# Expert tiles loaded four ahead in the first mixture, and the work beside them placed piece by piece inside tiles

## The chip, the cores and the metric

The kernel is one program on one core of one Trainium2 chip. The metric is the time of one execution on the device, in microseconds (us); lower is better. The core's engines each follow their own instruction stream: TensorE (PE, with its weight loads as PEld), VectorE (DVE), ScalarE (ACT), GpSimd (POOL) and SyncE (SP), which issues most of the transfers. They meet at semaphores.

## The reference, cut to what matters

Two layers follow each other on 4096 tokens (64 sequences of 64) of 256 numbers. Each has a sequence part (a scan and attention in the first; a recurrent net and a Mamba block in the second), whose result is added to x, and a feed-forward part. The change lies in the second layer's feed-forward part, two mixtures of experts in a row. The first has a shared part for all tokens and eight routed experts with GELU, of which each token takes two; the second has eight experts with SiLU gates, again two for each token:

```python
def _L1_cond2_ref(x, t_emb, W_router, router_bias, s_w1, s_w3, s_w2, r_w1, r_w2):
    for e in range(N_SHARED):                      # 2
        h = silu(x_flat @ s_w1[e].T) * (x_flat @ s_w3[e].T)
        shared_out = shared_out + h @ s_w2[e].T
    shared_out = shared_out / N_SHARED
    s = sigmoid(concatenate([x_flat, t_flat]) @ W_router.T)
    _, topk_idx = top_k(s + router_bias, TOP_K)    # 2 of 8
    s_sel = take_along_axis(s, topk_idx, axis=1)
    gates = s_sel / (sum(s_sel) + 1e-09)
    for e in range(N_EXPERTS):                     # 8
        h = gelu(x_flat @ r_w1[e].T, approximate=False)
        routed_out = routed_out + h @ r_w2[e].T * gates_full[:, e:e + 1]
    return (shared_out + routed_out) / (N_SHARED + TOP_K)

def _L1_ffn_ref(x, Wg, W1, W2, W3):
    topk_scores, topk_idx = top_k(xt @ Wg.T, TOP_K)      # 2 of 8
    gate = silu(einsum('td,ehd->teh', xt, W1))
    y = einsum('teh,edh->ted', gate * einsum('td,ehd->teh', xt, W2), W3)
    return einsum('te,ted->td', w, y)              # w: the two scores

x = x + _L1_attn_ref(_L1_cond_ref(x, ...), ...)
x = x + _L1_ffn_ref(_L1_cond2_ref(x, ...), ...)
return x
```

## The kernel before

Tokens are worked on in 8 chunks of 512. A mixture computes only the chosen experts: a token's row (its 256 numbers with weights, rank and number beside them) is written twice by POOL, with an indirect transfer, into the region of each of its experts (`Routing.send`, L1133, into `moe_x` or `ffn_x`). SP then loads a tile of 256 or 128 consecutive rows of one region (`Routing.read`, L1142, `gx`), with that expert's weights, chosen by a number that SP reads from a table. A tile goes through three steps on PE: `turn` (transposes of gx, L1330, copied to gxT by DVE, L1332), `up` (first products and the activation on ACT: `Gelu.up` L1421 and L1423, `Swiglu.up` L1463 to L1471) and `down` (second products, L1355, scaled by ACT at L1357). POOL scatters the result rows back by token (`give`, L1149, into `moe_y` or `ffn_y`).

The first mixture has two routings, moe0 for chunks 0 to 3 and moe1 for chunks 4 to 7, each with 16 full tiles (256 rows) and 8 half tiles (128 rows) in the order full, full, half: 48 tiles. The second has one routing for all chunks; its first 8 tiles (EARLY) come from a table made before the choice for chunks 4 to 7 is known, from what the first four chunks have sent.

All orders are written by hand. `Experts.run` is a generator: tile k+1 is turned and tile k+2's loads are issued between up and down of tile k, so loads run two tiles ahead, in pools of three buffers (`qw`, `gw`). It pauses once a tile, before up. Other work is cut in pieces by generators of its own, and `mixtures` decides how many pieces run between two tiles:

- Beside the first tiles: `Mixture.shared` for the last chunk (L1598, L1614), and `Mixture.rest`: scores of the last chunk, the choice for moe1, and the sends of chunks 4 to 7 (transposes L1580, then scatters). `send` pauses after every four scatters.
- From moe1's fourth tile on: the second mixture's gate for chunks 0 to 3. For a chunk, SP fetches the shared rows and the routed rows (L1158), DVE adds them (L1640), PE transposes the sum (L1664), ACT copies it to x2T, PE makes the scores (L1282, L1292); after every second chunk (a lot) DVE chooses the experts, two small matmuls count (L1099, L1100), and POOL scatters the lot's rows into ffn_x.
- Before the last three Gelu tiles the table of early Swiglu tiles is made (a count matmul at L1203) and Swiglu's generator is started; then the gate for chunks 4 to 7 runs between the first Swiglu tiles.

`scores`, which the gate and the mixtures use, is also used during Mamba, where pieces of the mixture's shared work and sends run beside the scans (VectorE, L916). There ACT switches between tables of functions (L884 exponentials, L762 and L1609 SiLU).

At the end the rows in ffn_y are loaded by chunks of 1 MB (`rows3`, three buffers), summed in pairs and transposed on PE (L1782), added to x by DVE (L1791) and stored.

Of the kernel before, what the change touches and what calls it, by code (L numbers as in the profile page):

```python
# [20 lines left out]
P = 128  # L21
# [1254 lines left out]
def scores(g, work, W, x, bias=None):  # L1276


    nc = g.nc
    ps = bank(g)  # L1280
    for k in range(KD):
        nc.tensor.matmul(ps[:NE, :], W[:, k, :], x[:, k, :], start=(k == 0), stop=(k == KD - 1))  # L1282
    s = work.tile([P, 2, CH // 2], F32, name="up").rearrange("p a (b l) -> p (a b) l", l=L)[:NE]
    pb = ps[:NE, :].rearrange("e (b l) -> e b l", l=L)
    if bias is None:
        nc.scalar.copy(s, pb)
    else:
        nc.vector.tensor_tensor(s, pb, bias.unsqueeze(2).to_broadcast([NE, CB, L]), ALU.add)
    s2 = s.rearrange("e b l -> e (b l)")
    pt = bank(g, (P, TT, NE))  # L1290
    for t in range(TT):
        nc.tensor.transpose(pt[:, t, :], s2[:, ts(t, P)], g.ident[:NE, :NE])  # L1292
    return pt


class Experts:
# [8 lines left out]
    def run(self, sections):  # L1305

# [64 lines left out]
        now = next(tiles)  # L1371
        load_rows(now)
        after = next(tiles)
        load_rows(after)
        turn(now)
        while now:
            yield
            self.up(now)
            if after:
                turn(after)  # L1380
            nxt = next(tiles, None)
            if nxt:
                load_rows(nxt)
            down(now)
            now, after = after, nxt
# [16 lines left out]
class Gelu(Experts):  # L1402


# [10 lines left out]
    def up(self, v):  # L1415
        nc = self.g.nc
        n = self.H // P
        ps = bank(self.g, (P, n, TR))[:, :, : v.rows]
        for j in range(n):
            for k in range(KD):  # L1420
                nc.tensor.matmul(ps[:, j, :], v.w1[:, k, ts(j, P)], v.xT[:, k, :], start=(k == 0), stop=(k == KD - 1))  # L1421
        v.h = self.p2.tile([P, n, TR], F32, name="rh")[:, :, : v.rows]
        nc.scalar.activation(v.h, ps, AF.Gelu)  # L1423

# [4 lines left out]
class Swiglu(Experts):  # L1429

# [19 lines left out]
    def up(self, v):  # L1453
# [3 lines left out]
        for i in range(full + 1):  # L1457
# [10 lines left out]
            else:  # L1468
# [6 lines left out]
                for j in range(v.S):  # L1475
                    nc.vector.tensor_mul(v.h[ts(j, H2), i, ts(j, P)], s[H2:, ts(j, P)], ps[H2:, 0, ts(j, P)])

# [9 lines left out]
class Mixture:  # L1487
# [31 lines left out]
    def beside(self, c, x, work):  # L1519

        g = self.g
        pt = scores(g, work, self.Wr[:, :KD, :], x, self.cond[:, ts(c, CB)])
        g.nc.scalar.copy(self.score[:, ts(c, TT), :], pt)
        yield
        if c == MLOT - 1:
            yield from self.choose(0, work)
        for i in self.SENDS.get(c, ()):
            yield from self.send(i, work, work)  # L1530
        if c == NCH - 2:
            self.tables = self.routings[0].tiles(self.pool)
            yield
        yield from self.shared(c, x, work)
# [88 lines left out]
    def rest(self, x, work, pool):  # L1623

        pt = scores(self.g, work, self.Wr[:, :KD, :], x, self.cond[:, (NCH - 1) * CB :])
# [6 lines left out]
    def combine(self, c, rows, work):  # L1632

        nc = self.g.nc
        nc.sync.dma_start(rows, self.made[ts(c, CH), :].rearrange("(t p) d -> p t d", p=P))
        got = work.tile([P, TT, 2, D], F32, name="rows2")
        self.routings[c // MLOT].fetch(c, got)
        yield
        for j in range(2):
            nc.vector.tensor_add(rows, rows, got[:, :, j, :])  # L1640


class Gate:
# [13 lines left out]
    def chunk(self, c, rows, work):  # L1657

        g, nc = self.g, self.g.nc
        x = work.tile([P, KD, CH], F32, name="x2T")  # L1660
# [6 lines left out]
        pt = scores(g, work, self.Wg, x)  # L1667
# [25 lines left out]
def mixtures(g, mix, x, out, last, work, close):  # L1693
# [7 lines left out]
    some = lambda pieces, n: deque(islice(pieces, n), 0)  # L1701
    with ExitStack() as ctx:
# [3 lines left out]
        first, q2, q3, qy = pool("qw", 3), pool("q2", 2), pool("q3", 2), pool("qy", 6)  # L1706
# [6 lines left out]
        n += NHT  # L1713
        others, shared = mix.rest(last, work, q3), mix.shared(NCH - 1, last, work)
        for _ in range(4):
            some(others, 1)
            some(shared, 3)
        for i in range(n - 1):
            next(tiles)
            some(others, 2)  # L1720
            some(shared, 2)
# [3 lines left out]
        next(tiles)  # L1725
        close()

        pw, p2, p3, py = pool("gw", 3), pool("g2", 2), pool("g3", 3), pool("gy", 4)
# [3 lines left out]
        def gates(chunks):  # L1732
            for c in chunks:
                rows = pg.tile([P, TT, RW], F32, name=f"x2_{c % MLOT}")
                yield from mix.combine(c, rows[:, :, :D], pg2)
                yield from gate.chunk(c, rows, pg)
# [9 lines left out]
        )  # L1746
        others = gates(range(MLOT))
        for i in range(n):
            if i > 3:
                some(others, 2)  # L1750
            if i == n - 3:
                some(others, None)
                tables2.append(routing.early(p1))
                next(tiles2)
            next(tiles, None)
        others = gates(range(MLOT, NCH))
        for i in range(EARLY - 2):
            some(others, 1 if i == 0 else 6)
            next(tiles2)
# [4 lines left out]
        next(tiles2)  # L1764
        px, close_px = scoped(tc, "gx", side="right")
        xs = []
        for c in range(NCH):
            x = px.tile([P, KD, CH], F32, name=f"x3_{c}")
            nc.sync.dma_start(x, g.x[:, :, ts(c, CH)])
            xs.append(x)  # L1770
            some(tiles2, 1)
        some(tiles2, None)
        for c in range(NCH):
            rows = px.tile([P, TT, 2, D], F32, name=f"rows3_{c % 3}")
# [161 lines left out]
```

## Time and profile before

| what | value |
|---|---|
| runs | 3056.66, 3058.62, 3066.81 us; median 3058.62 |
| profiled execution | 3053.17 us, of which the span of its instructions is 3051.3 |
| mean granted clock of TensorE | 0.907 |
| PE busy with the shared experts' first products (L1598) | 256.4 us in 896 matmuls |
| PE busy with Gelu down (L1355, tiles of r) | 86.5 us in 316 matmuls |
| PE busy with Swiglu up (L1463) | 326.6 us in 1600 matmuls |
| VectorE's scans in Mamba (L916) | 603.1 us in 512 instructions |
| POOL's scatters of Gelu results (L1149, moe_y) | 76.7 us in 79 instructions, 971 ns each |
| ACT_TABLE_LOAD at L884 | 61.6 us in 48, 1283 ns each |

In the span's own time, the layers up to the recurrent net take 0 to 827 us, Mamba 827 to 2059, the first mixture with its neighbours 2059 to about 2438, the first Swiglu tiles with the last gate chunks to 2550, the other Swiglu tiles to 2995, and the tail the rest.

In a row of an engine's timeline the first number is the start, the second the time the group of instructions took, then engine, line, operation, output and inputs, shapes and count; in square brackets stands the idle time of that engine just before, and what ended it. "Remote" means a semaphore that the trace doesn't tie to one instruction, "issue" time in which the engine waited for nothing that the profile shows. A share of the span is a mean over stages with different limits, so the table is read by stage.

### The profile page before, as it was taken

How to read it: one execution, taken by the hardware profiler on the slowest of the kernel's cores; microseconds unless marked ns; L12 is line 12 of the kernel's file. 1: busy time of each engine (PE TensorE's matmuls, PEld its weight loads, DVE VectorE, ACT ScalarE, POOL GpSimd, SP SyncE). 2: the span in 40 equal slices, each digit the busy share in tenths (PEclk: the TensorE clock that was granted, in tenths of full speed). 3: DMA queues.
4: the chain of work that ended last, by engine and by line, in shares of the span. 5: the costliest groups of instructions: out<-in, count | busy, mean ns of one | idle time of the engine just before them, and what ended most of it. 6: DMA issues, size and time to landing. Idle time of an engine off the chain costs nothing.

```text
span 3051.3 us, 39241 instructions
## 1 busy us (share of the span) xinstructions
PE 2476.9 (81%) x13958; PEld 1767.9 (58%) x13958; DVE 1789.2 (59%) x3013; ACT 1403.2 (46%) x2397; POOL 1305.2 (43%) x1116
## 2 busy tenths in 40 slices
PE   3888885778957778888788888788975789999996
PEld 3544443446724455565555555566754567888885
DVE  0565547884059988898988888872242333332332
ACT  0554435775356585857484857443321221222220
POOL 0021114541056766777577868755434232111110
PEclk9999987879766899999899999899987899999998
DMA  9996010000011212121222121315665847566655
GB/s 207 371 347 235 1 45 24 18 18 18 14 56 63 83 60 73 60 80 60 66 66 94 60 100 57 114 45 169 201 224 158 280 151 241 188 212 201 211 186 174
DMA packets 243716, 383.62 MB, mean 126 GB/s; under 512 B 36305, under 2 KB 144593, under 8 KB 243265
## 3 DMA queue, kind: packets, MB, share of 16 engines
q1 hardware_dynamic: 230128, 344.27, 35.2%
q0 software_dynamic: 13392, 36.85, 3.2%
q8 instruction: 110, 1.80, 0.2%
q14 instruction: 86, 0.70, 0.1%
HBM read 258.21 MB, written 122.83 MB: 125 GB/s over the span
## 4 chain that ended last, share of the span: by engine, by line
PE 46%; DVE 22%; ACT 11%; issue 7%; DMA 4%; POOL 4%; SPq 3%; another core or an unknown queue 2%; DVEq 0%; POOLq 0%; ACTq 0%
DVE hb L916 11%; PE ps L1463 10%; PE acc L1355 7%; PE acc L379 4%; DVE hb L918 3%; PE yp L932 2%; PE mq L1598 2%; PE mq L1614 2%; DVE xc L758 2%; PE ps L1421 1%; PE mp L813 1%; PE ps L652 1%; PE ps L535 1%; PE acc L652 1%
## 5 line engine op out<-in xcount | busy, mean ns | idle before, releaser
L877 POOL TENSOR_TENSOR hb<-dx,Bn 128x1024 f32<-128x1024 f32 x256 | 601.3, 2358 | 259.4 <-PE yp L932 247.8
L916 DVE TENSOR_TENSOR_SCAN hb<-dA,hb 128x512 f32<-128x512 f32 x512 | 603.1, 1210 | 34.8 <-ACT dA L884 32.3
L884 ACT ACTIVATE dA<-delta,A 128x504 f32<-128x504 f32 x512 | 344.1, 683 | 287.2 <-DVE hb L916 282.8
L932 PEld LDWEIGHTS yp<-ident,hb 128*128 128x128 f32 x2048 | 269.5, 153 | 163.2 <-issue 124.7
L918 DVE TENSOR_TENSOR hb<-hb,cb 128x1024 f32<-128x1024 f32 x256 | 312.3, 1220 | 72.1 <-PE cb L829 55.7
L1463 PE MATMUL ps<-gxT,w 128*128 128x256 f32 (+1 forms) x1600 | 326.6, 363 | 5.9 <-issue 5.7
L1463 PEld LDWEIGHTS ps<-gxT,w 128*128 128x128 f32 x1600 | 278.5, 191 | 51.0 <-issue 19.1
L932 PE MATMUL yp<-ident,hb 128*128 128x128 f32 x2048 | 304.0, 293 | 0.0
L1598 PE MATMUL mq<-x,moe_s 128*128 128x256 f32 x896 | 256.4, 421 | 49.6 <-ACT up L1605 25.0
L1149 POOL DMA_INDIRECT ffn_y<-gy,to x72 | 69.0, 959 | 465.6 <-ACT gy L1357 398.7
L1598 PEld LDWEIGHTS mq<-x,moe_s 128*128 128x128 f32 x896 | 174.6, 210 | 111.6 <-ACT up L1605 31.5
L1357 ACT ACTIVATE gy<-acc,wt 128x256 f32<-128x256 f32 x151 | 66.8, 472 | 306.2 <-PE acc L1355 223.2
L1355 PE MATMUL acc<-w,gh 128*128 128x256 f32 (+1 forms) x864 | 187.6, 388 | 0.5 <-DVE gh L1467 0.5
L1467 DVE TENSOR_TENSOR gh<-gs,ps 128x256 f32<-128x256 f32 (+1 forms) x200 | 78.2, 393 | 185.9 <-ACT gs L1466 175.8
L829 PE MATMUL cb<-parts,pick 80*128 80x512 bf16 x256 | 105.7, 413 | 98.5 <-DVE hb L918 82.9
L1466 ACT ACTIVATE gs<-ps 128x256 f32<-128x256 f32 (+1 forms) x200 | 71.9, 362 | 230.2 <-PE ps L1463 213.3
L361 POOL TENSOR_TENSOR E<-E,z 128x1024 f32<-128x1024 f32 x32 | 60.8, 1901 | 270.6 <-DVE z L360 171.7
L1355 PEld LDWEIGHTS acc<-w,gh 128*128 128x128 f32 (+1 forms) x864 | 145.5, 189 | 30.8 <-issue 10.8
L1149 POOL DMA_INDIRECT moe_y<-gy,to x79 | 76.7, 971 | 145.7 <-ACT gy L1357 123.1
L379 PE MATMUL acc<-oT,Wout 128*128 128x512 f32 x256 | 114.2, 605 | 7.9 <-ACT oT L373 7.9
L1355 PE MATMUL acc<-r,rh 128*128 128x256 f32 x316 | 86.5, 416 | 41.2 <-issue 21.8
L1614 PE MATMUL mq<-moe_s,sh 128*128 128x256 f32 x448 | 113.1, 390 | 5.8 <-ACT up L1605 5.8
(452 smaller groups left out, 4618.9 us busy)
## 6 DMA issues: line engine op xcount, KB each, us to landing
Bn<-B SPq DMA_DIRECT2D x128, 512.0 KB
w<-in_ffn_W_dram SPq DMA_DIRECT2D x80, 640.0 KB
moe_x<-fill SPq DMA_DIRECT2D x130, 260.0 KB
ffn_x<-fill SPq DMA_DIRECT2D x129, 260.0 KB
w<-in_ffn_W_dram SPq DMA_DIRECT2D x40, 704.0 KB
r<-in_moe_r_dram SPq DMA_DIRECT2D x96, 256.0 KB
gx<-moe_x SPq DMA_DIRECT2D x32, 260.0 KB
gx<-ffn_x SPq DMA_DIRECT2D x32, 260.0 KB
```

The costliest lines, as they stand in the source:

```text
L379: nc.tensor.matmul(ps, wa.Wout[:, o, ts(k, P)], v.o[:, o], start=(o == 0), stop=(o == H // 2 - 1))
L829: nc.tensor.matmul(t, pick[:, n : n + 1].to_broadcast([rows, P]), v.parts, start=True, stop=True)
L877: nc.gpsimd.tensor_mul(hb, vs[c].dx[p], Bn[:, n % NB, :].unsqueeze(1).to_broadcast([P, PI, CH]))
L884: nc.scalar.activation(decays[s][i][:, :, 1:], seq(vs[c].delta[p][:, i, :])[:, :, 1:], AF.Exp, scale=w.A[:, p * PI + i, n : n + 1],)
L916: ins = nc.vector.tensor_tensor_scan(h, dA[i].rearrange("p b l -> p (b l)"), h, 0.0, ALU.mult, ALU.add)
L918: ins = nc.vector.tensor_tensor(hb, hb, cb.unsqueeze(1).to_broadcast([P, PI, CH]), ALU.mult)
L932: nc.tensor.matmul(yp[i][:, t, :], hb[:, i, ts(t, P)], g.ident, start=(n == 0 and t == 0), stop=(n == S - 1 and t == CH // P - 1), is_tran ...
L1149: i = self.g.nc.gpsimd.indirect_dma_start(out=self.y, out_offset=bass.IndirectOffsetOnAxis(ap=to, axis=0), in_=y, in_offset=None)
L1355: nc.tensor.matmul(po[s], h, w, start=(i == 0), stop=(i == n - 1))
L1463: nc.tensor.matmul(ps[:, j, :], v.w12[:, k, ts(j * (full + 1) + i, P)], v.xT[:, k, :], start=(k == 0), stop=(k == KD - 1))
L1598: nc.tensor.matmul(ps[:, i % 2, :], w[:, k, ts(i, P)], xu[:, k, :], start=(k == 0), stop=(k == KD - 1))
L1614: nc.tensor.matmul(ps[:, t, :], h[:, i, ts(t, P)], self.s2[:, i, :], start=(i == 0), stop=(i == NS - 1))
```

## The change

`Experts.run` keeps the tiles that are loaded in a queue: four ahead for Gelu (its pool `qw` has five buffers), two ahead for Swiglu (three buffers, as before). It pauses at more places: after the first loads, before up (with a mark, TILE), at six places inside a Swiglu up, between turn and down, and after down. A new helper, `tiles_on`, runs n tiles and takes one piece of each neighbour's work at each pause. Five pieces of `rest` and 15 of `shared` stand ahead of the first tile, for four and 12. All 48 Gelu tiles run to their end; before, the last was started but its up and down were never reached.

Swiglu's generator is started ahead of the last Gelu tiles, as before, but its first step now only loads; its first transposes come after the last Gelu tile. The gate's row fetches are a step of their own, issued one chunk ahead, and `x2T` lies in a pool with two buffers. `scores` pauses once more, in Mamba too. The tail has two buffers of result rows for three, and one load of x for each of the last Swiglu tiles. In the changed file most of the lines named above stand further down: L1330 is 1335, L1421 is 1434, L1463 is 1479, L1640 is 1658, L1664 is 1682, L1782 is 1815.

```diff
--- before.py
+++ after.py
@@ -1286,6 +1286,7 @@
         nc.scalar.copy(s, pb)
     else:
         nc.vector.tensor_tensor(s, pb, bias.unsqueeze(2).to_broadcast([NE, CB, L]), ALU.add)
+    yield
     s2 = s.rearrange("e b l -> e (b l)")
     pt = bank(g, (P, TT, NE))
     for t in range(TT):
@@ -1293,6 +1294,9 @@
     return pt
 
 
+TILE = "tile"
+
+
 class Experts:
 
 
@@ -1303,6 +1307,7 @@
         self.p2, self.p3, self.py, self.pw = pools
 
     def run(self, sections):
+
 
 
 
@@ -1368,21 +1373,27 @@
                         yield load(routing, table, rank, n + j, HR, sent)
 
         tiles = order()
-        now = next(tiles)
-        load_rows(now)
-        after = next(tiles)
-        load_rows(after)
-        turn(now)
-        while now:
+        ahead = deque()
+
+        def more():
+            for v in islice(tiles, 1):
+                load_rows(v)
+                ahead.append(v)
+
+        for _ in range(self.AHEAD):
+            more()
+        yield
+        turn(ahead[0])
+        while ahead:
+            yield TILE
+            now = ahead.popleft()
+            yield from self.up(now)
+            if ahead:
+                turn(ahead[0])
+            more()
             yield
-            self.up(now)
-            if after:
-                turn(after)
-            nxt = next(tiles, None)
-            if nxt:
-                load_rows(nxt)
             down(now)
-            now, after = after, nxt
+            yield
 
 
 def in_order(tc, ap, engines, most):
@@ -1402,6 +1413,8 @@
 class Gelu(Experts):
 
 
+    AHEAD = 4
+
     def weights(self, v, e):
         nc, a = self.g.nc, self.g.a
         self.H = H = a["moe_r1"].shape[1] // NE
@@ -1421,6 +1434,7 @@
                 nc.tensor.matmul(ps[:, j, :], v.w1[:, k, ts(j, P)], v.xT[:, k, :], start=(k == 0), stop=(k == KD - 1))
         v.h = self.p2.tile([P, n, TR], F32, name="rh")[:, :, : v.rows]
         nc.scalar.activation(v.h, ps, AF.Gelu)
+        return ()
 
     def parts(self, v, s):
         return [(v.h[:, j, ts(s, P)], v.w2[:, j, :]) for j in range(self.H // P)]
@@ -1430,6 +1444,8 @@
 
 
 
+
+    AHEAD = 2
 
     def weights(self, v, e):
         nc, a, pool = self.g.nc, self.g.a, self.pw
@@ -1474,6 +1490,7 @@
                 nc.scalar.activation(s[H2:, :], ps[:H2, 0, :], AF.Silu)
                 for j in range(v.S):
                     nc.vector.tensor_mul(v.h[ts(j, H2), i, ts(j, P)], s[H2:, ts(j, P)], ps[H2:, 0, ts(j, P)])
+            yield
 
     def parts(self, v, s):
         got = [(v.h[:, i, ts(s, P)], v.w3[:, i, :]) for i in range(self.full)]
@@ -1521,7 +1538,7 @@
 
 
         g = self.g
-        pt = scores(g, work, self.Wr[:, :KD, :], x, self.cond[:, ts(c, CB)])
+        pt = yield from scores(g, work, self.Wr[:, :KD, :], x, self.cond[:, ts(c, CB)])
         g.nc.scalar.copy(self.score[:, ts(c, TT), :], pt)
         yield
         if c == MLOT - 1:
@@ -1622,22 +1639,23 @@
 
     def rest(self, x, work, pool):
 
-        pt = scores(self.g, work, self.Wr[:, :KD, :], x, self.cond[:, (NCH - 1) * CB :])
+        pt = yield from scores(self.g, work, self.Wr[:, :KD, :], x, self.cond[:, (NCH - 1) * CB :])
         self.g.nc.scalar.copy(self.score[:, (NCH - 1) * TT :, :], pt)
         yield
         yield from self.choose(1, work)
         for c in range(MLOT, NCH):
             yield from self.send(c, work, pool, x if c == NCH - 1 else None)
 
-    def combine(self, c, rows, work):
-
-        nc = self.g.nc
-        nc.sync.dma_start(rows, self.made[ts(c, CH), :].rearrange("(t p) d -> p t d", p=P))
+    def fetch(self, c, rows, work):
+
+        self.g.nc.sync.dma_start(rows, self.made[ts(c, CH), :].rearrange("(t p) d -> p t d", p=P))
         got = work.tile([P, TT, 2, D], F32, name="rows2")
         self.routings[c // MLOT].fetch(c, got)
-        yield
+        return got
+
+    def combine(self, rows, got):
         for j in range(2):
-            nc.vector.tensor_add(rows, rows, got[:, :, j, :])
+            self.g.nc.vector.tensor_add(rows, rows, got[:, :, j, :])
 
 
 class Gate:
@@ -1654,17 +1672,17 @@
 
     LOT = 2
 
-    def chunk(self, c, rows, work):
+    def chunk(self, c, rows, work, work2):
 
         g, nc = self.g, self.g.nc
-        x = work.tile([P, KD, CH], F32, name="x2T")
+        x = work2.tile([P, KD, CH], F32, name="x2T")
         for k in range(KD):
             ps = bank(g)
             for t in range(TT):
                 nc.tensor.transpose(ps[:, ts(t, P)], rows[:, t, ts(k, P)], g.ident)
             nc.scalar.copy(x[:, k, :], ps)
         yield
-        pt = scores(g, work, self.Wg, x)
+        pt = yield from scores(g, work, self.Wg, x)
         nc.scalar.copy(self.score[:, ts(c, TT), :], pt)
         self.rows[c] = rows
         yield
@@ -1699,11 +1717,21 @@
 
     nc, tc = g.nc, g.tc
     some = lambda pieces, n: deque(islice(pieces, n), 0)
+
+    def tiles_on(tiles, n, *beside):
+
+        for mark in tiles:
+            n -= mark is TILE
+            if n == 0:
+                break
+            for pieces in beside:
+                some(pieces, 1)
+
     with ExitStack() as ctx:
         pool = lambda name, bufs: ctx.enter_context(tc.tile_pool(name=name, bufs=bufs))
         p1 = pool("e1", 1)
         gate = Gate(g, p1, x)
-        first, q2, q3, qy = pool("qw", 3), pool("q2", 2), pool("q3", 2), pool("qy", 6)
+        first, q2, q3, qy = pool("qw", Gelu.AHEAD + 1), pool("q2", 2), pool("q3", 2), pool("qy", 6)
         moe0, moe1 = mix.routings
         n = moe0.ntl
         tables1 = []
@@ -1711,29 +1739,37 @@
             [(moe0, lambda: mix.tables, n, NHT, None), (moe1, lambda: tables1[0], n, NHT, None)]
         )
         n += NHT
+        next(tiles)
         others, shared = mix.rest(last, work, q3), mix.shared(NCH - 1, last, work)
-        for _ in range(4):
+        for _ in range(5):
             some(others, 1)
             some(shared, 3)
-        for i in range(n - 1):
-            next(tiles)
-            some(others, 2)
-            some(shared, 2)
+        tiles_on(tiles, n - Gelu.AHEAD + 1, others, shared)
         some(others, None)
         some(shared, None)
         tables1.append(moe1.tiles(p1))
-        next(tiles)
         close()
 
-        pw, p2, p3, py = pool("gw", 3), pool("g2", 2), pool("g3", 3), pool("gy", 4)
+        pw, p2, p3, py = pool("gw", Swiglu.AHEAD + 1), pool("g2", 2), pool("g3", 3), pool("gy", 4)
         pg, close_pg = scoped(tc, "gate", side="right")
         pg2, close_pg2 = scoped(tc, "gate2", side="right", bufs=2)
 
         def gates(chunks):
+            got = {}
+
+            def fetch(c):
+                rows = pg.tile([P, TT, RW], F32, name=f"x2_{c % MLOT}")
+                got[c] = rows, mix.fetch(c, rows[:, :, :D], pg2)
+
+            fetch(chunks[0])
+            yield
             for c in chunks:
-                rows = pg.tile([P, TT, RW], F32, name=f"x2_{c % MLOT}")
-                yield from mix.combine(c, rows[:, :, :D], pg2)
-                yield from gate.chunk(c, rows, pg)
+                if c + 1 in chunks:
+                    fetch(c + 1)
+                    yield
+                rows, routed = got.pop(c)
+                mix.combine(rows[:, :, :D], routed)
+                yield from gate.chunk(c, rows, pg, pg2)
 
         routing = gate.routing
         ntl = routing.ntl - EARLY
@@ -1744,34 +1780,31 @@
                 (routing, lambda: tables2[1], ntl, NHT, None),
             ]
         )
+
+        tiles_on(tiles, Gelu.AHEAD + 3)
         others = gates(range(MLOT))
-        for i in range(n):
-            if i > 3:
-                some(others, 2)
-            if i == n - 3:
-                some(others, None)
-                tables2.append(routing.early(p1))
-                next(tiles2)
-            next(tiles, None)
+        tiles_on(tiles, n - 7, others)
+        some(others, None)
+        tables2.append(routing.early(p1))
+        next(tiles2)
+        some(tiles, None)
         others = gates(range(MLOT, NCH))
-        for i in range(EARLY - 2):
-            some(others, 1 if i == 0 else 6)
-            next(tiles2)
+        some(tiles2, 7)
+        tiles_on(tiles2, EARLY - Swiglu.AHEAD, others)
         some(others, None)
         close_pg2()
         close_pg()
         tables2.append(routing.tiles(p1))
-        next(tiles2)
         px, close_px = scoped(tc, "gx", side="right")
         xs = []
         for c in range(NCH):
+            tiles_on(tiles2, 1)
             x = px.tile([P, KD, CH], F32, name=f"x3_{c}")
             nc.sync.dma_start(x, g.x[:, :, ts(c, CH)])
             xs.append(x)
-            some(tiles2, 1)
         some(tiles2, None)
         for c in range(NCH):
-            rows = px.tile([P, TT, 2, D], F32, name=f"rows3_{c % 3}")
+            rows = px.tile([P, TT, 2, D], F32, name=f"rows3_{c % 2}")
             routing.fetch(c, rows)
             x = xs[c]
             for k in range(KD):
```

## The prediction

> **What bounds the kernel now.** I read the busy table and the slices first, then busy time by stage, then TensorE's own timeline where a stage has idle time, and last the other engines' timelines at the gaps.
>
> ```profile
> PE 2476.9 (81%) x13958; PEld 1767.9 (58%) x13958; DVE 1789.2 (59%) x3013; ACT 1403.2 (46%) x2397; POOL 1305.2 (43%) x1116
> PE   3888885778957778888788888788975789999996
> PEclk9999987879766899999899999899987899999998
> ```
>
> The slices show where the change can act: at slices 30 to 32 the PE digits fall to 7, 5, 7 and the granted clock to 7 and 8, between mamba, which VectorE bounds (its scans are the first line of the chain), and the last stage, where PE is full.
>
> ```profile
> 2059.00:2222.00 163.00, 139.23 (x666) 115.67 (x667) 52.44 (x269) 56.02 (x99) 81.96 (x92) 0.94 0.61 188
> 2222.00:2300.00 78.00, 47.58 (x203) 35.01 (x202) 28.64 (x113) 16.00 (x35) 29.56 (x34) 0.83 0.67 219
> 2300.00:2362.00 62.00, 40.38 (x158) 28.08 (x157) 16.32 (x84) 12.85 (x29) 27.18 (x30) 0.78 0.47 145
> 2362.00:2438.00 76.00, 53.96 (x241) 40.72 (x239) 26.26 (x116) 17.95 (x37) 17.11 (x22) 0.87 0.84 274
> 2438.00:2550.00 112.00, 93.01 (x423) 72.90 (x423) 39.30 (x154) 21.05 (x57) 40.97 (x45) 0.92 0.57 190
> 2550.00:2995.00 445.00, 445.00 (x2265) 379.31 (x2264) 136.38 (x503) 95.07 (x255) 54.80 (x58) 1.00 0.59 194
> ```
>
> After the window's bounds come its length, then busy time of PE, weight loads, DVE, ACT and POOL, the granted clock, DMA share and GB/s. From 2059 to 2550 PE is busy 374.2 of 491 us, so 116.8 us are idle; from 2550 it is never idle, and loading ahead can win nothing there. PE's timeline gives the idle pieces:
>
> ```profile
> 2226.74 1.11 PE L1330 MATMUL ps<-ident,gx 128*128 128x128 f32 x4 [4.17 <-DMA gx<-moe_x]
> 2228.64 3.71 PE L1421 MATMUL ps<-gxT,r 128*128 128x256 f32 x8 [0.78 <-DVE gxT L1332]
> 2234.93 1.89 PE L1421 MATMUL ps<-gxT,r 128*128 128x256 f32 x8
> 2246.91 1.94 PE L1664 MATMUL ps<-ident,x 128*128 128x128 f32 x8 [4.80 <-DVE x L1640]
> 2298.28 2.08 PE L1355 MATMUL acc<-r,rh 128*128 128x256 f32 x4 [13.34 <-issue]
> 2378.32 0.17 PE L1203 MATMUL ps<-total,ffn_onesb 128*128 128x8 bf16 x1
> 2394.34 1.09 PE L1330 MATMUL ps<-ident,gx 128*128 128x128 f32 x4 [13.34 <-DMA gx<-ffn_x]
> 2395.22 1.91 PE L1421 MATMUL ps<-gxT,r 128*128 128x128 f32 x8
> 2432.34 1.06 PE L1664 MATMUL ps<-ident,x 128*128 128x128 f32 x8 [2.84 <-DVE x L1640]
> ```
>
> Two kinds stand here: late data (gx, the combined rows x) and one gap "on issue", which nothing on PE explains. POOL and DVE explain that one:
>
> ```profile
> 2275.94 0.98 POOL L1133 DMA_INDIRECT ffn_x<-x,ffn_row  x1 [0.57 <-POOL ffn_row L1108]
> 2299.92 0.96 POOL L1133 DMA_INDIRECT ffn_x<-x,ffn_row  x1 [0.30 <-issue]
> 2304.09 0.69 DVE L1332 COPY gxT<-ps 128x512 f32<-128x512 f32 x1 [16.23 <-remote]
> 2479.80 0.84 ACT L1357 ACTIVATE gy<-acc,wt 128x256 f32<-128x256 f32 x2 [13.82 <-remote]
> ```
>
> POOL issues 20 scatters in a row, one every 1.26 us, from 2275.94 to 2300.9. DVE, whose input PE finished before 2285, starts at 2304.09, 3.2 us after the last scatter. The same is seen around three more bursts (2332–2357, 2457–2477, 2509–2529): hand-offs from PE are held from some 8 to 11 us into the burst until about 3 us after it. PE's idle there is 13.34+2.77, then 7.45+3.83+3.33, then 10.36+1.07, then 5.7 in small pieces, and about 13 in 2108–2137 with the scatters of the first sends: 61 us of the 116.8.
>
> **The change, part by part.** The sum is a difference from the profiled execution (3053.17 us, span 3051.3), which is 5.45 below the median 3058.62; I add the difference to the median.
>
> *Gelu tiles loaded four ahead.* The first tile of the second routing is awaited at 2226.74: 4.17 us, and its first up takes 3.71 for the usual 1.89. Two more tiles of lead are about 8 us, so the wait goes: −5.5 of 6.0 (bounds −6 and, if the load is held elsewhere on SP, 0).
>
> *The first two Swiglu tiles are loaded, but no longer turned, before the last Gelu tiles.* Before, Swiglu's first transposes stand on PE ahead of Gelu tiles 44 and 45 and wait 13.34. The tables come from the counts at 2378.32; gx is there at 2394.34, 16.0 us later. In the new order PE has down 43 (1.99), half tile 44, full 45 and 46, half 47 ahead of those transposes. A full tile is 0.43 transposes + 1.73 up + 1.73 down = 3.9 busy, a half one 1.95; undisturbed triples (full, full, half) take 12.0 for 9.75, which is 0.75 idle a tile. So 2.0+2.7+4.65+4.65+2.7 = 16.7 us cover 16.0. Gain 13.34, and the cold work behind it: 1.09+1.91+1.06+1.85 for 0.60+1.05+0.60+1.13, 2.5. I take −15; if SP issued those loads 5 us later, −10; that is the lower bound.
>
> The Trainium skill ("TensorE: Matmul & The Clock Gate", Part 1: The HAM clock gate) has a rule for this cold work: an idle window of about 3.4 us halves the array's clock, and some 3.4 us of work restore it. By it a removed long gap would return 1.7 us beside itself, where the rows give 1.8 and 2.5, and every gap that the change lengthens past 3.4 us would cost 1.7 more; the sum would move by less than 1 us. The rows are used.
>
> *Gate chunks 4–7 inside Swiglu tiles, rows fetched a chunk earlier.* Before, two chunks stand alone on PE from 2425.07 to 2438.18, 13.1 us for 7.6 of work at full clock (two chunks of 8 transposes 1.06, 4 score matmuls 1.88, 4 small transposes 0.41, with their ends), and the next two take 9.0 for 7.6 at 2481–2490. Now each piece has eight or more matmuls of 363 ns behind it, and the 2.84 for DVE's adds goes. −7 (bounds −7 and −4, where the adds still queue on DVE).
>
> *Pieces inside Gelu tiles.* In 2059–2222 PE idles 163.0−139.2 = 23.8, less the sends' 13 leaves 10.8 for up and down waiting on ACT and DVE in some 22 tiles, 0.5 each. A piece between up and down covers it in the 12 tiles that still have pieces: −4 (0 to −6). But shared work now ends by tile 12 and not 18, so six more tiles run bare at 0.75 each: +4.5. One half tile that the run before never reaches (47 tiles have an up, now 48) is +2.5.
>
> *First gate chunks.* The five-deep buffers make tile 31's gx take tile 26's buffer, and the rows fetch of chunk 0 stands behind that load on SP; behind it in turn wait weights and gx of tiles 32 on, which have four tiles of lead. It can issue only after up 26. Its landing and the two adds take 6.52+2.5, with the issue 10 to 12 us; PE is at that place one tile of 4.4 later. The old wait of 4.80 with its cold start grows by +2 (bounds −5, adds covered by the next tile, and +6). The next chunks' fetches are a chunk ahead and covered. The count matmul (L1099) waited 3.76 for the choice on DVE, which takes 6.6 us from the scores; one tile lies between now, and more of DVE's work: +3.5 (0 to +4).
>
> *scores() pauses once more.* In mamba this moves pieces among ACT's table switches: the program has 127 table loads for 121, at 1283 ns, 7.7 us of ACT. ACT is off the limit mostly: the chain holds about 23 of the 61.6 us of L884's table loads, 38%, so +3 (0 to +7.7; the cover is DVE's scan lead).
>
> *Tail.* The result rows go through two buffers for three. Loads land in 5.75 to 6.29 us each, one after another, and PE's share is 2 to 3.6 a chunk, so the load, not the buffer, sets the pace: +1 (0 to +5).
>
> *The scatters.* Their number stays; pieces of four stand singly, but three per tile where there were two, and a tile of 4.7 us frees POOL for only four scatters, so POOL stays behind: the changed program's instruction order on POOL still has 8 + 8 and 16 scatters straight. 0, with −30 and +31 as bounds, worked out below.
>
> Sum: −5.5 −15 −7 −4 +4.5 +2.5 +2 +3.5 +3 +1 = −15.0. Forecast 3058.62−15 = 3043.6.
>
> **The rivals.** *(1) The bursts break up.* A stall is about burst length less 8 us (bursts of 25, 25, 20 and 20 us gave 16.1, 14.6, 11.4 and 5.7, the last with long runs of Swiglu matmuls queued). If a tile's work comes between every four scatters, no burst reaches 8 us and the whole 61 us go, 2983; if half of them do, 3043.6−30 = 3014. For: singly placed pieces. Against: POOL's order in the new program, above.
>
> *(2) Bursts merge (slower).* Three pieces per tile ask for up to 12 scatters, 15 us, per 4.7 us tile. If two lots' 16 run as 32, the burst lasts 40.5 and holds PE 32.5. For the first two lots that replaces 30.7, +2; for the two of the Swiglu stage it replaces 17.1, +15; and the second mixture half's sends, two chunks with tile scatters between, 28 in a row or 35 us, hold 27 for 13, +14. All together +31: 3058.6−15+31 = 3075. It is slower than can be told from no change once the merging costs over 24. For: the first sends now end by tile 6 instead of 8. Against: PE itself stops in a burst, so the next lot can hardly be chosen before the burst is over.
>
> *(3) The gain doesn't arrive.* Swiglu's early loads are late (−10), the rows fetch +6, table loads +7.7, two tail buffers +5, bare tiles as above: −15+5+4+4.7+4 = +2.7, 3061. For: the 23 us of table loads on the chain. Against: the 13.34 gap loses its cause in the instruction order itself.
>
> **How the numbers follow.** About 0.3% (9.2 us) can be told from no change here, so faster is below 3049.4, slower above 3067.8. Forecast 0.45 (own range 3032 to 3052, faster in nearly all of it), rival 1 0.13, rival 2 0.23, rival 3 0.19. Faster 0.13+0.43 = 0.56, same 0.02+0.17+0.02 = 0.21 with a weak merging, slower 0.21+0.02 = 0.23. The range runs from rival 1's 3014 to rival 2's 3075, and leaves out a full break-up and worse mergers.
>
> **What would show it.** In the profile after: no gap on gx<-ffn_x before the first Swiglu transposes and none on gx<-moe_x at the change of routing; no serial chunks near the start of Swiglu; gaps on "issue" or "remote" with the scatter bursts still there; the wait for the combined rows at the first gate chunk some 2 us longer; the first Swiglu-only stage still 100% PE. Wrong if the mamba stage moves by more than 8 us either way, if bursts are gone, or if the Swiglu loads land after Gelu tile 47.

## The result, and the profile after

The changed kernel takes 3064.31 us (median of 12 runs, 3048.74 to 3069.13) against 3058.3 us (12 runs, 3054.4 to 3066.81) before: a ratio of 1.0009, interval 0.9995 to 1.0024. That is no change that can be told. Forecast was 3043.6, 15 us less.

The two profiled executions show where the gain went. Mamba ends here with VectorE's last addition of a result (L857). The mixtures end where PE's instruction stream reaches the first semaphore of the tail's matmuls (L1782, in the changed file L1815), some 2 us before the last Swiglu matmul is over.

| stage | before, us | after, us | difference |
|---|---|---|---|
| up to Mamba's first scan | 875.9 | 876.4 | +0.5 |
| Mamba, first scan to last result | 1177.8 | 1206.6 | +28.8 |
| mixtures | 946.2 | 922.8 | -23.4 |
| tail | 51.4 | 57.1 | +5.7 |
| span | 3051.3 | 3062.8 | +11.5 |

The mixtures, which the change is about, gave more than forecast (the terms of the sum that lie there come to -19.0). Mamba, where the change only adds one pause per chunk, took it back. First the mixtures: busy time by window of the changed kernel, with the columns as before (bounds and length, then PE, weight loads, DVE, ACT, POOL, the granted clock, DMA share, GB/s).

```profile
2083.00:2260.00 177.00, 148.66 (x719) 123.28 (x718) 58.15 (x295) 57.37 (x101) 82.47 (x93) 0.93 0.62 201
2260.00:2320.00 60.00, 40.00 (x191) 28.33 (x189) 28.53 (x109) 16.17 (x36) 24.42 (x28) 0.87 0.77 249
2320.00:2380.00 60.00, 33.22 (x137) 23.91 (x136) 13.90 (x70) 10.70 (x25) 31.11 (x34) 0.76 0.50 160
2380.00:2414.00 34.00, 31.08 (x153) 25.46 (x152) 13.59 (x77) 11.12 (x23) 14.22 (x19) 0.96 0.74 246
2414.00:2560.00 146.00, 123.77 (x550) 95.78 (x551) 54.91 (x211) 30.24 (x76) 44.91 (x49) 0.91 0.55 188
2560.00:3005.00 445.00, 445.00 (x2282) 379.79 (x2281) 133.80 (x483) 96.24 (x258) 56.62 (x59) 1.00 0.61 204
```

From Mamba's end to the Swiglu-only stage PE now idles 477.0-376.7 = 100.3 us; before it was 116.8 from 2059. The window ahead of the first Swiglu tile (2380 to 2414) is nearly full (31.08 of 34 us), and the stage from 2560 still has no idle time. PE's own timeline at the places of the prediction, in the changed kernel:

```profile
2280.49 1.94 PE L1682 MATMUL ps<-ident,x 128*128 128x128 f32 x8 [8.47 <-DVE x L1658]
2344.02 0.20 PE L1099 MATMUL ps<-both,ffn_before 128*128 128x64 bf16 x1 [1.60 <-DVE both L1085]
2370.85 2.07 PE L1360 MATMUL acc<-r,rh 128*128 128x256 f32 x4 [13.55 <-issue]
2397.97 0.17 PE L1203 MATMUL ps<-total,ffn_onesb 128*128 128x8 bf16 x1
2414.79 0.60 PE L1335 MATMUL ps<-ident,gx 128*128 128x128 f32 x4
2416.17 4.15 PE L1479 MATMUL ps<-gxT,w 128*128 128x256 f32 x18 [0.78 <-DVE gxT L1337]
2434.92 1.94 PE L1682 MATMUL ps<-ident,x 128*128 128x128 f32 x8 [3.59 <-DVE x L1658]
```

From the counts (L1203) to Swiglu's first transposes are 16.8 us of Gelu tiles with no gap over 0.6, where before stood 13.34 of idle time. The wait for the first combined rows is 8.47 for 4.80. A gap on "issue" beside a scatter burst is still there, 13.55.

Now Mamba. These are the scans and their partner on VectorE (cb is made for it by a matmul, L829), one of ScalarE's table loads, ScalarE's copies for the shared experts (L1605, in the changed file L1622), and a count for the first routing's table of tiles (L1205), from the groups of instructions in Mamba's stretch; before first, then the changed kernel. After the bar stand the busy time, the mean ns of one, and the idle time before the group with what ended it.

```profile
L916 DVE TENSOR_TENSOR_SCAN hb<-dA,hb 128x512 f32<-128x512 f32 x512 | 603.1, 1210 | 34.8 <-ACT dA L884 32.3 <-POOL hb L877 2.2
L918 DVE TENSOR_TENSOR hb<-hb,cb 128x1024 f32<-128x1024 f32 x256 | 312.3, 1220 | 72.1 <-PE cb L829 55.7
L884 ACT ACT_TABLE_LOAD x48 | 61.6, 1283 | 0.8
L1605 ACT COPY up<-mq 128x512 f32<-128x512 f32 x56 | 32.6, 582 | 21.7 <-PE mq L1598 11.9 <-POOL sh L1606 9.8
L1205 DVE COPY n_e<-mq 128x8 f32<-128x8 f32 x1 | 0.2, 166 | 0.1
```

```profile
L916 DVE TENSOR_TENSOR_SCAN hb<-dA,hb 128x512 f32<-128x512 f32 x512 | 602.9, 1208 | 48.2 <-ACT dA L884 45.7 <-POOL hb L877 2.2
L918 DVE TENSOR_TENSOR hb<-hb,cb 128x1024 f32<-128x1024 f32 x256 | 312.1, 1219 | 82.0 <-PE cb L829 63.9 <-DVE hb L916 0.5
L884 ACT ACT_TABLE_LOAD x51 | 65.4, 1283 | 0.9
L1622 ACT COPY up<-mq 128x512 f32<-128x512 f32 x56 | 32.6, 582 | 40.3 <-PE mq L1615 21.6 <-POOL sh L1623 18.6
L1205 DVE COPY n_e<-mq 128x8 f32<-128x8 f32 x1 | 0.2, 166 | 8.3 <-PE mq L1203 8.3
```

VectorE does the same work in the same time (in all of Mamba it is busy 1030.7 us before and 1030.4 after), so the 28.8 us are waiting. It waits 13.4 us more for the decays dA and 8.2 more for cb, and 8.3 at one new place, for the counts n_e, where it did not wait before; small waits go up and down by a few us. How a wait for dA comes about can be read at one scan step of the last chunk but one, in the timeline of the changed kernel:

```profile
1772.84 1.25 POOL L1623 TENSOR_TENSOR sh<-sh,up 128x512 f32<-128x512 f32 x1
1774.06 2.35 POOL L877 TENSOR_TENSOR hb<-dx,Bn 128x1024 f32<-128x1024 f32 x1
1774.12 0.59 ACT L1622 COPY up<-mq 128x512 f32<-128x512 f32 x1 [4.69 <-POOL sh L1623]
1774.61 1.90 ACT L884 ACTIVATE dA<-delta,A 128x504 f32<-128x504 f32 x3
1774.76 1.67 PE L1615 MATMUL mq<-x,moe_s 128*128 128x256 f32 x4 [3.56 <-ACT up L1622]
1775.40 2.34 DVE L916 TENSOR_TENSOR_SCAN hb<-dA,hb 128x512 f32<-128x512 f32 x2 [3.39 <-ACT dA L884]
```

Here two pieces of the shared experts (L1622, L1623) meet Mamba's own products on POOL. ACT's copy waits 4.69 for POOL; the exponentials that the next scan needs stand behind that copy in ACT's queue; the scan starts 3.39 late. Nothing in these lines is new work. The pieces stand one place later than before. Over all of Mamba these copies wait 18.6 us for POOL where they waited 9.8. Where one pause is added to the kernel before (e2, below) it is 18.9, and with the places put back (e3) 10.7.

### The profile page after: what moved, and what is told of

Same layout as the page of the kernel before. It is cut to its first block, busy times and chain, and to the rows that moved or that the text cites. A ratio compares the mean times of both kernels' runs of the same rounds, so it can differ in the third digit from the quotient of the medians.

```text
span 3062.8 us, 39271 instructions
## 1 busy us (share of the span) xinstructions
PE 2480.3 (81%) x13970; PEld 1769.4 (58%) x13970; DVE 1790.9 (58%) x3013; ACT 1414.6 (46%) x2405; POOL 1306.5 (43%) x1117
## 4 chain that ended last, share of the span: by engine, by line
PE 48%; DVE 21%; ACT 13%; issue 7%; POOL 4%; DMA 3%; another core or an unknown queue 3%; SPq 1%; DVEq 0%; ACTq 0%; POOLq 0%
DVE hb L916 11%; PE ps L1479 10%; PE acc L1360 8%; PE acc L379 4%; DVE hb L918 2%; PE mq L1615 2%; PE ps L1434 2%; PE yp L932 2%; PE mp L813 1%; DVE xc L758 1%; PE ps L652 1%; POOL hb L877 1%; ACT dA L884 1%; PE ps L535 1%
## 5 line engine op out<-in xcount | busy, mean ns | idle before, releaser
L916 DVE TENSOR_TENSOR_SCAN hb<-dA,hb 128x512 f32<-128x512 f32 x512 | 602.9, 1208 | 48.2 <-ACT dA L884 45.7
L829 PE MATMUL cb<-parts,pick 80*128 80x512 bf16 x256 | 106.3, 415 | 89.1 <-DVE hb L918 72.5
L1360 PEld LDWEIGHTS acc<-w,gh 128*128 128x128 f32 (+1 forms) x864 | 148.3, 192 | 30.8 <-issue 10.9
L1350 DVE TENSOR_REDUCE wt<-pick 128x2 f32<-128x4 f32 (+1 forms) x88 | 13.6, 156 | 190.4 <-ACT gy L1362 173.2
L1337 DVE COPY gxT<-ps 128x512 f32<-128x512 f32 (+1 forms) x88 | 54.3, 617 | 105.3 <-remote 60.3
```

The source lines that it names most:

```text
L829: nc.tensor.matmul(t, pick[:, n : n + 1].to_broadcast([rows, P]), v.parts, start=True, stop=True)
L916: ins = nc.vector.tensor_tensor_scan(h, dA[i].rearrange("p b l -> p (b l)"), h, 0.0, ALU.mult, ALU.add)
L1360: nc.tensor.matmul(po[s], h, w, start=(i == 0), stop=(i == n - 1))
```

## The experiments

All twelve ran where the kernel before takes 3005 to 3008 us (medians 3007.92, 3007.29 and 3005.14 of three groups, e1 to e4, e6 to e9 and e10 to e13, each on a chip of its own), some 50 us less than in the first comparison. So times are compared by ratio to the kernel before of the same group, and stages between these runs alone. A run's own edit can move the line numbers: L916 is L917 in e3. There the stretch of the mixtures is 893.9 us with the order of before (e2, e7: 893.5) and 875.7 with that of the change (e10).

**The pause taken out of Mamba.** `whole` runs a generator to its end.

```diff
-        pt = yield from scores(g, work, self.Wr[:, :KD, :], x, self.cond[:, ts(c, CB)])
+        pt = whole(scores(g, work, self.Wr[:, :KD, :], x, self.cond[:, ts(c, CB)]))
```

> The changed kernel, except that the scores made beside Mamba run in one piece again; every other pause stays. Theory A (the extra pause of scores() shifts every later piece beside Mamba by one place and costs the 29.3 us by which Mamba's last result came later, 2082.9 for 2053.6): that result is back at about 2054, the end at 3062.8-29 = 3034 (time about 3036), ACT table loads back near 121. Rival B (Mamba grew from something else in the change, such as where pools lie or how the program is loaded, or varies by itself between executions): the result stays near 2083 and the time near 3064. Rival C (what Mamba gives back is lost again in the mixtures): result at 2054, the time above 3055.

Measured: 2993.32 us, 0.9953 of before (0.9938 to 0.9968), 14.6 us less. Mamba takes 1181.2 us, with 121 table loads in the program. Theory A holds. The rest of the change is worth 14.6 us (by the interval 10 to 19), where the forecast without its Mamba term was 18.0.

**The pause alone, in the kernel before.**

```diff
@@ scores
+    yield
     s2 = s.rearrange("e b l -> e (b l)")
@@ Mixture.beside (the other two callers run it through whole)
-        pt = scores(g, work, self.Wr[:, :KD, :], x, self.cond[:, ts(c, CB)])
+        pt = yield from scores(g, work, self.Wr[:, :KD, :], x, self.cond[:, ts(c, CB)])
```

> The kernel before, with the extra pause of scores() beside Mamba alone; the scores of the last chunk and of the gate run in one piece. Theory A: Mamba's last result 25 to 30 us later than before (2054 to about 2082), the time about 3086. Rival B: no change, 3058. Where A holds half (the mixture part hides some of it) 3070 to 3080.

Measured: 3030.96 us, 1.0082 (1.0063 to 1.0101), 23 us more. Mamba takes 1204.4, against 1181.1 and 1177.8 in two other kernels with the old pieces (e7, e13). One `yield` costs 23 to 27 us in this kernel.

**The pause kept, the places put back.**

```diff
                 others = beside(c, x)
+                next(others)
```

> The changed kernel with the pause kept, but the first piece beside Mamba is taken at once when a chunk's generator is made, so that all later pieces stand in the places they had before the change. If theory A's cause is the shift of places (which piece lands at which scan step), Mamba's last result is back within 5 us of 2054 and the time at 3036 to 3042. If it is the split of the scores itself (their second half late, more ACT table loads by the split), most of the 29 us stays and the time is 3055 to 3065.

Measured: 2989.97 us, 0.9935 (0.9919 to 0.9952). Mamba takes 1173.9 us, the least of all runs so far, with the scores split in two. The table loads are back at 121 and VectorE's wait for n_e is gone. The cost lies in the places at which the later pieces land, not in the split. How much each of the waits adds is not separated by any run. VectorE's wait for dA is 33.4 here and 45.0 in e2:

```profile
L917 DVE TENSOR_TENSOR_SCAN hb<-dA,hb 128x512 f32<-128x512 f32 x512 | 603.4, 1210 | 36.1 <-ACT dA L885 33.4 <-POOL hb L878 2.2
```

```profile
L916 DVE TENSOR_TENSOR_SCAN hb<-dA,hb 128x512 f32<-128x512 f32 x512 | 603.4, 1210 | 47.5 <-ACT dA L884 45.0 <-POOL hb L877 2.2
```

**Three buffers in the tail.**

```diff
-            rows = px.tile([P, TT, 2, D], F32, name=f"rows3_{c % 2}")
+            rows = px.tile([P, TT, 2, D], F32, name=f"rows3_{c % 3}")
```

> As e1 with three buffers for the result rows of the tail instead of two; to make room the last chunk's x goes into the first chunk's place and is loaded in the tail. From the end of the last Swiglu up to the end of the span took 51.6 us before and 57.1 in the changed kernel (first tail matmul to end 51.5 and 57.1). If two buffers cost the 5.6 us, the tail is 5 to 6 us shorter than in e1 and the time about 3031; if it is the two executions' transfers that differ, no difference beyond 2 us.

Measured: 2990.13 us, 0.9941 (0.9924 to 0.9957), beside e1's 0.9953: the intervals overlap. The tail takes 51.6 us, e1's 56.6. But with two buffers it took 52.8 to 57.1 in the runs of this study. The kernel before, with three, has 50.4 to 51.4 in four profiles. So a cost of two buffers is not shown apart from these swings: three took 51.6 here and 55.8 in e12.

**The pieces between tiles.** As e3; `tiles_on` counts the pauses and runs the pieces owed at the next TILE mark.

```diff
+            owed += 1
+            if mark is TILE:
+                for _ in range(owed):
+                    for pieces in beside:
+                        some(pieces, 1)
+                owed = 0
```

> As e3_pause_realigned (0.9935 of before there, -18 us), but the pieces are saved up and run together ahead of an up, between tiles, with the same number per tile and the same order; four tiles ahead and the other edits stay. If placing pieces singly inside tiles is worth what the prediction's sum gave it (-4 for filled gaps, -7 for gate chunks inside Swiglu), this is 8 to 11 us slower than e3, about 0.997 of before. If the place inside a tile does not matter because the engines' queues run ahead anyway, it is within 3 us of e3.

Measured: 3006.24 us, 0.9996 (0.9985 to 1.0007), e3 having 0.9935: 18 us, more than expected. In the profiles the mixtures take 893.6 for 882.1, so 11.5 of it are seen there; the tail is 3 us longer too, which is within its swings.

**Swiglu's transposes late, alone.** In the kernel before:

```diff
         load_rows(after)
+        yield
         turn(now)
@@ mixtures, one more next() ahead of each generator's first tile
+        next(tiles)
...
+        next(tiles2)
```

> The kernel before with one edit: the first step of Swiglu's generator only loads, and its first transposes come after the last Gelu tile that runs (47 tiles as before, two ahead, pieces between tiles, no pause in the scores). The prediction's largest term, -15 (13.34 idle and 2.5 cold): expected 0.995 of before, and no wait for gx<-ffn_x over 3 us ahead of the first Swiglu transposes. If the wait only moves (the Gelu tiles are over before gx lands, or weights of the last Gelu tiles stand behind Swiglu's on SP), -5 or less.

Measured: 3010.61 us, 1.0014 (1.0004 to 1.0024). The expected gain is not there, and the profile shows where the wait went, on PE and on SP's queue:

```profile
2372.46 1.11 PE L1330 MATMUL ps<-ident,gx 128*128 128x128 f32 x4 [16.15 <-DMA gx<-moe_x]
```

```profile
2355.82 0.38 SPq L1142 DMA_DIRECT2D gx<-ffn_x  x1
...
2363.19 0.38 SPq L1142 DMA_DIRECT2D gx<-ffn_x  x1
...
2366.80 0.37 SPq L1142 DMA_DIRECT2D gx<-moe_x  x1
```

The wait is for a Gelu tile's gx now (moe_x). SP issues both Swiglu tiles' weights and rows first, and those wait for the table; the last Gelu tiles' loads come behind them. So the edit can pay only if these Gelu tiles are loaded before, which is what four ahead does; the next run tests it.

**Two ahead.** As e3 with `AHEAD = 2` in Gelu.

> As e3 with Gelu tiles loaded two ahead in three buffers, and nothing else changed. Theory A (the lead itself is worth the first moe1 tile's 6 us, and frees the tiles from short waits for weights): 5 to 8 us slower than e3. Rival B (the lead costs about as much as it gives, since the five-deep buffers put the gate's first row fetch behind later loads, 8.5 us of wait in the changed kernel for 4.8 before): within 3 us of e3, with the wait for the combined rows back at about 5 and the wait at the change of routing back at about 4.

Measured: 3004.38 us, 0.9988 (0.9978 to 0.9997), 16 us over e3 by the ratios, twice what was expected. The wait at the change of routing is back (3.92 <-DMA gx<-moe_x), and so is that ahead of Swiglu (15.24 <-DMA gx<-moe_x), while the first row fetch costs nothing over 2 us. The gain of the late transposes goes with the lead, which the expectation did not count.

**The row fetches in written order.** As e3.

```diff
-        self.g.nc.sync.dma_start(rows, self.made[ts(c, CH), :].rearrange("(t p) d -> p t d", p=P))
+        i = self.g.nc.sync.dma_start(rows, self.made[ts(c, CH), :].rearrange("(t p) d -> p t d", p=P))
+        self.g.tc.keep_in_program_order(i)
```

> As e3, with the fetch of a chunk's shared rows kept in the written order on SP. Without that the scheduler puts the fetches for chunks 4 to 7 among the Gelu loads, where each waits until the scatters have read chunk 0 to 3's buffer, with the Gelu tiles' weights and rows queued behind it. Theory S (part of the idle time at the scatter bursts is SP held by these fetches): the 15 us gap of e3 near the second lot's choice (2288 to 2304) falls under 6 and the time is 8 to 15 us less than e3. Theory H of the prediction (hand-offs held by the burst itself, whatever SP does): the gap stays over 10, time within 4 us of e3.

Measured: 2982.73 us, 0.9917 (0.99 to 0.9933), 5 us under e3 by the ratios, where 8 to 15 were expected; the intervals overlap. In the profiles the mixtures take 874.6 for 882.1. The two kernels at the second lot's choice, e3 first:

```profile
2281.91 0.37 SPq L1652 DMA_DIRECT2D x<-shared_rows  x1
2282.98 0.37 SPq L1424 DMA_DIRECT2D r<-in_moe_r_dram  x1
2293.58 0.37 SPq L1652 DMA_DIRECT2D x<-shared_rows  x1
...
2296.03 0.35 SPq L1143 DMA_DIRECT2D gx<-moe_x  x1
```

```profile
2303.65 0.23 PE L1100 MATMUL ps<-both,ffn_before 128*128 128x64 bf16 x1 [15.08 <-DVE both L1086]
```

```profile
2290.66 0.20 PE L1100 MATMUL ps<-both,ffn_before 128*128 128x64 bf16 x1 [1.59 <-DVE both L1086]
```

In e3 SP issues nothing from 2283.4 to 2293.6: the fetch of a later chunk's rows stands there, waiting for the scatters that still read its buffer, and the next Gelu tile's gx stands behind it. With the order kept the 15.08 is 1.59, so theory S holds for the gap. The mixtures gain less than the gap, because PE's gap at the next burst grows from 5.44 to 11.03 us. This is VectorE there in e9:

```profile
2325.35 0.20 DVE L1348 TENSOR_TENSOR to<-at,pick 128x2 int32<-128x2 f32 x1 [11.09 <-DMA moe_y<-gy,to]
2325.47 0.68 DVE L1338 COPY gxT<-ps 128x512 f32<-128x512 f32 x1
```

VectorE may not write a tile's addresses until the scatter of the tile six back has read the same buffer, and that scatter stands in POOL's queue behind 16 to ffn_x. gxT, which PE needs, stands behind the addresses on VectorE.

**The changed kernel once more**, beside the next three.

> The changed kernel as it is, beside the other runs of this call. From the parts measured so far: the pause beside Mamba +23 (1.0082 alone), the rest of the change -14 to -18 (0.9953 without the pause): the sum is +5 to +9, 1.002 to 1.003 of before. If the two parts do not add (the later Mamba end hides or frees something in the mixture), it is outside 0.999 to 1.005.

Measured: 3015.99 us, 1.0043 (1.0029 to 1.0057): 10.9 us more, just over the expected 5 to 9. Mamba takes 1203.4 us, the mixtures 875.7. Within the interval the two parts add. The ratio is above the 1.0009 of the first comparison: the change takes 18.2 us off the mixtures here (875.7 for 893.9) and took 23.4 there.

**A longer ring of result buffers.** As e9.

```diff
-        first, q2, q3, qy = pool("qw", Gelu.AHEAD + 1), pool("q2", 2), pool("q3", 2), pool("qy", 6)
+        first, q2, q3, qy = pool("qw", Gelu.AHEAD + 1), pool("q2", 2), pool("q3", 2), pool("qy", 8)
```

> As e9, with eight buffers instead of six for a tile's result rows and their addresses. In e9 VectorE waits 11.1 us at 2325.4 before it may write a tile's addresses, because the scatter that reads the buffer's former content (moe_y, six tiles back) stands behind 16 scatters to ffn_x on GpSimd, and PE's up waits 11.0 behind it. Theory R (the ring of six sets how long a burst may last before PE stands): two more tiles are 8 to 9 us, the gap at the second lot's burst falls to about 3 and the time by 6 to 9 us, to about 0.989 of before. Theory H of the prediction (hand-offs held by the burst whatever the buffers): the gap stays and the time is within 3 us of e9.

Measured: 2978.74 us, 0.992 (0.9903 to 0.9936), not told apart from e9. VectorE's wait for the addresses is 9.06 for 11.09 and PE's gap behind it 8.7 for 11.0, where about 3 was expected. The mixtures take 866.2 for 874.6, but the tail 55.8 for 53.0. The wait still ends some 4 us after the burst of 16 scatters does, as in e9: POOL is as far behind as before, and the longer ring lets PE arrive earlier at the same wait.

**Combined.** As e11, with three tail buffers (the last two chunks' x loaded there), and

```diff
             fetch(chunks[0])
-            yield
+            for _ in range(4 if chunks[0] == 0 else 5):
+                yield
```

> As e11, with three buffers of result rows in the tail (the last two chunks' x loaded there), and the gate's first work delayed by three places in the Gelu tiles and four in Swiglu's, so that the combined rows are there: in e9 PE waits 11.0 us for them at 2234.7 and 5.3 at 2374.2. Expected: those waits near 6 and 2, the tail 1 to 3 us shorter, the time 6 to 11 us under e11, about 0.986 of before. If the work only moves into a later wait, within 3 us of e11.

Measured: 2972.65 us, 0.9894 (0.9878 to 0.9911), 32.5 us under before: the fastest of all, 6.1 us under e11 and faster than both kernels of this study. The waits for the combined rows are 4.8 and under 2 (8.7 and 5.0 in e11); the tail did not get shorter.

**The longer ring in the kernel before.** Eight result buffers and 14 for the addresses, six each before.

> The kernel before with eight buffers for result rows and 14 for their addresses (6 and 6 before), nothing else. Theory R: its tiles take longer beside the bursts and its waits there were 5 to 7 us on this chip, for gx behind SP, not for the ring: within 4 us of before, 0.999 to 1.001. If the ring is what holds before's PE at the bursts, 5 to 15 us less.

Measured: 2992.76 us, 0.996 (0.9949 to 0.997), 12.4 us less. No more than 4 was expected; the size is that of the other theory, that the ring holds PE at the bursts. But PE's waits at the Gelu bursts are still there (5.5 and 4.2 us, for gx). The mixtures take 882.2 against 893.9; a wait of 7.5 us inside Swiglu, seen in e2 and e7 behind VectorE, is not among e13's gaps over 2 us. What the rest is made of stays open. Longer rings alone give the old order about as much (0.996) as the whole change gives without its pause in Mamba (0.9953).

## Why the prediction was wrong

The step that failed is "scores() pauses once more", +3 with bounds 0 to +7.7. Those bounds were made from the six table loads alone, ACT's 7.7 us. The step named the real event, "this moves pieces among ACT's table switches", but priced only the switches, and let VectorE's scan lead cover most of them. The shift itself puts every later piece one place off, on ACT, POOL and PE, in seven chunks, and the lead does not cover that: VectorE waits longer for dA, cb and n_e. It costs 28.8 us in the profile of the result, 23 us alone (e2), nothing if the places are put back (e3). Put in for the +3, it turns -15.0 into +10.8, near the profiled +11.5 (+6.0 by the medians). That the other terms come out so near their sum is in part luck: the mixtures gave 23.4 for 19.0, and the tail took 5.7 for 1.

- *Four ahead at the change of routing*, -5.5: the wait went as forecast; its size was not measured apart. No wait for gx<-moe_x stands there after; with two ahead it is back at 3.92 (e8).
- *Swiglu turned after the Gelu tiles*, -15: the wait and its cover were right, counting it by itself was wrong. The 13.34 are gone; the cover was forecast at 16.7 and is 16.8. But alone the edit gains nothing (e7), and with two tiles ahead a wait of 15.24 stands in its place (e8). Four ahead without the edit was not tried.
- *Pieces inside tiles and gate chunks inside Swiglu*, -4 and -7: right in direction; together 11.5 in the profiles and 18 by the ratios (e6).
- *First row fetch*, +2: it is +3.7 (8.47 for 4.80). *The count matmul's wait*, +3.5: it fell instead, to nothing from 3.76 in the first lot and to 1.60 from 1.99 in the second.
- *Bare tiles, the half tile*: not measured apart. *Tail*, +1: +5.7 in the profile of the result, just outside its bound of 5, and not shown to come from the buffers (e4).
- *The scatters*, 0: the gaps stay, so rival 1 (bursts break up) is out, and nothing shows a merging, rival 2. The reason given for the gaps, hand-offs held by the burst itself, fits the two profiles of the first comparison alone. In e3 the gap is SP's queue held by a row fetch, and in e9 VectorE held by the ring of address buffers.
- Rival 3 came near the measured time with its 3061, by luck: Swiglu's loads were not late, and its 4.7 for the table loads is not the 25.8 that Mamba cost beyond the forecast.

The forecast also put 0.56 on faster. Its test, "wrong if the mamba stage moves by more than 8 us either way", was the place where it broke.

## What to carry to other kernels

Where small pieces of work are dealt out by count beside a tight loop, one more or fewer pause moves all that follow, and the loop's engines meet them at other steps: price such an edit by a run, or compare the order of the instructions step by step in the loop, however little it adds. A helper that is used in two places carries a change into both; look at every caller's stage. A wait that is taken off PE by reordering is gone only if the work put ahead of it is loaded already; look at the load queue's order first.

## What the runs showed of the hardware

The same program differs by 50 us between the place of the first comparison and that of the experiments, with almost the same granted clock (0.907 in the profile of before, 0.905 to 0.914 in that kernel's executions there). The difference lies in the mixtures (946.2 us, and 893.9 with the same order in e2). In the first, VectorE's copies and ScalarE's scaling wait on "remote" beside the bursts. In the mixtures of all twelve experiments no wait of VectorE or ScalarE is on "remote", though POOL issues the same scatters every 1.27 us. The changed kernel itself has 60.3 us of them ahead of gxT in the first place and none in e10. VectorE's copy of the transposes in both, first the kernel before, then e2:

```profile
L1332 DVE COPY gxT<-ps 128x512 f32<-128x512 f32 (+1 forms) x56 | 34.4, 614 | 104.7 <-PE ps L1330 47.5 <-remote 41.9 <-issue 7.5
```

```profile
L1342 DVE COPY gxT<-ps 128x512 f32<-128x512 f32 (+1 forms) x57 | 35.0, 614 | 53.0 <-PE ps L1340 51.0 <-PE ps L1203 1.3 <-issue 0.2
```

So the scatters alone do not hold these hand-offs; something in which the two places differ has a part in it. No run here shows what it is, and the cause stays open.
